# A two-layer graph attention block: the short last node tile spreads its two output halves over all four column groups of the array

## The chip, the cores and the metric

The kernel runs on one core of one Trainium2 chip. The metric is the device time of one execution in microseconds (us). Three runs of the kernel before gave 1805.76, 1805.07 and 1804.87 us: median 1805.07 us.

Short names used below: PE is TensorE (PEld its weight loads), DVE is VectorE, ACT is ScalarE, POOL is GpSimd, SP is SyncE, which only issues transfers here. A "row" of the profile is one line of it. A column group is a strip of 32 of the array's 128 columns; a matmul with up to 32 output rows occupies one strip, and its result lands in the 32 PSUM partitions of that strip.

## The reference

3125 nodes with 768 features, 53125 edges sorted by destination (25000 drawn ones in both directions and one self loop per node; the convolution adds a second self loop). All is fp32.

```python
h = relu(layernorm(x))
# layer 1: 4 heads of 256;  layer 2: 1 head of 768
def gat_conv(x, src, dst, W, a_src, a_dst, bias):
    xl = x @ W
    e = leaky_relu((xl @ a_src)[src] + (xl @ a_dst)[dst], 0.2)
    e = exp(e - segment_max(e, dst)[dst])
    alpha = e / (segment_sum(e, dst)[dst] + 1e-16)
    return segment_sum(xl[src] * alpha, dst) + bias
h1 = relu(layer_norm(gat_conv(h, W1 ...))) + h @ Wr1 + br1
h2 = layer_norm(gat_conv(h1, W2 ...)) + h1 @ Wr2 + br2
out = x + h2
```

## The kernel before

The nodes are cut into 25 tiles: tiles 0 to 23 have 128 nodes, tile 24 has the remaining 53 (`rows_of`, L116). The edges of a node tile lie in 17 slot tiles of 128 edges, of which tile 24 uses 8 (`tiles_of`, L122). A slot tile j feeds one or two quarters of the node tile, that is 32 nodes each (`QUARTERS`, L33), and the slot tiles are taken in five rounds (`ROUNDS`, L34). For tile 24 these are the slot tiles (0, 5), (1, 6), (4), (2) and (3, 7); only slot tile 4 feeds two quarters, so 9 pairs of slot tile and quarter are left, against 20 in a full tile.

**Before layer 1's sums.** Products x W1 are stored to the table `table1` in DRAM, attention weights and slot lists are made, and a part of h Wr1 is computed ahead. The first row gather of layer 1 is issued at 496.77 us of the span.

**Layer 1** (`sums`, L633 to L745, with `end1`, L1123 to L1176). POOL gathers one row of 4 KB per edge from `table1` by an indirect DMA per slot tile (L692). For each round PE multiplies the 0/1 placement, scaled by the attention weight (`w`, made on DVE at L712 and L713), with the gathered tile `g` and accumulates in the PSUM tile `pa` (L732): four column ranges of 256 per pair, the first two in one PSUM bank (`pa[:, 0]`), the last two in the next. After each round `step` advances the node tiles that are already summed: `finish` (L655; normalisation on DVE, L663 to L670, after a lag of three rounds) and then `end1`: layer norm (L1134 to L1138), transposes on PE (L1145, in `flip`), ReLU on ACT (L1150), adding of the residual on DVE (L1152), store of h1 to DRAM (L1159), and the dense product with W2 (L1164 to L1170), 8 steps of 128 rows of W2 by two output halves of 384 and 386 columns, each half in a PSUM tile `p2` of its own. ACT copies the halves into a row (L1173), DVE a pair of attention values (L1175), and SP stores the rows to `table2` (L1176, `store_rows` at L194). Dense products go through `by_columns` (L178), which issues a matmul per 32 output rows: 4 for a full tile, 2 (32 and 21 rows) for tile 24. The order on PE, DVE and ACT is the order in which the code is written (`manual_schedule`): in the last part of layer 1 the rounds of tile 24 alternate on PE with transposes and product of tile 22; then come tiles 23 and 24 with nothing between.

**Layer 2** (L1181 to L1421). No row of `table2` can be gathered before tile 24's rows are stored. POOL then gathers 3 KB rows (L1280), up to 36 slot tiles ahead (`RING`). For tile b the softmax needs all its slot tiles (`values`, L1293; `softmax`, L1304, with transposes `mix` at L1311 and L1325), then come five rounds of sums (`summed`, L1332; matmuls at L1347, two halves of 384 columns in two PSUM banks), then `finish` (L1352): DVE L1360 to L1367, with a square root on ACT (L480) in between, and the store of the output. Between the rounds PE works on the dense residual product h1 Wr2 (`residuals`, L1244; again `by_columns`, two halves of 384 columns in PSUM tiles `pr0`, `pr1`), which runs three tiles ahead of the sums: that of tile 24 is computed during the rounds of tile 21. On DVE, all of `finish(23)` stands ahead of `finish(24)`: the loop empties `ending` at its third round (L1406), and L1360 of the new tile follows at the fifth (L1410).

In the trace each fp32 matmul of the program stands as two rows (two passes): 3136 rows for the products with W2 are 2 x (24 x 64 + 32).

Of the kernel before, what the change touches and what calls it, by code (L numbers as in the profile page):

```python
# [68 lines left out]
def in_order(  # L69
# [108 lines left out]
    def by_columns(out_, lhsT, rhs, m, start, stop):  # L178

        for o in range(0, m, 32):  # L180
            e = min(o + 32, m)
            nc.tensor.matmul(out_[o:e], lhsT[:, o:e], rhs, start=start, stop=stop, skip_group_check=True)  # L182
# [450 lines left out]
    def sums(heads, cols, table, al, alo_d, ahead, lag, gp, ap, pp, end, more, pace, first=None, delay=0.0):  # L633
# [21 lines left out]
        def finish(b, own, pa):  # L655
            for _ in range(lag):
                yield

            r = rows_of(b)
            v = gp.tile([P, 2, heads], F32, name="aw", bufs=3)[:r]  # L660
            aw, share = v[:, 0], v[:, 1]
            ao = asked.pop(b)[:r]
            nc.vector.tensor_scalar(aw, ao[:, :heads, b], has[:r, 1, b:b + 1], has[:r, 2, b:b + 1],  # L663
                                    op0=OP.mult, op1=OP.max)
            nc.vector.scalar_tensor_tensor(share, ao[:, heads:, b], has[:r, 0, b:b + 1], aw, op0=OP.mult, op1=OP.add)
            nc.vector.tensor_scalar(share, share, 1e-16, None, op0=OP.add)
            nc.vector.reciprocal(share, share)
            z = gp.tile([P, width], F32, name="z", bufs=2)[:r]
            for o in range(0, width, n):
                nc.vector.scalar_tensor_tensor(z[:, o:o + n], own[:r, o:o + n], aw[:r, o // cols:o // cols + 1],  # L670
                                               pa[:r, o // f, o % f:o % f + n], op0=OP.mult, op1=OP.add)
            yield from end(b, z, share)
# [44 lines left out]
        with tc.manual_schedule(engines={PE, ACT, DVE}):  # L717
            ready = fetch(0, 0)
            for b in range(NB):
# [3 lines left out]
                for k, js in enumerate(ROUNDS):  # L723
# [5 lines left out]
                    for o in range(0, width, n):  # L729
                        for q, w, g in made:  # L730
                            to = (o // f, q)
                            nc.tensor.matmul(pa[32 * q:32 * q + 32, o // f, o % f:o % f + n], w[:, o // cols, :],  # L732
                                             g[:, o:o + n], start=to not in opened, stop=False,
                                             skip_group_check=True)
                            opened.add(to)
# [12 lines left out]
    with tc.tile_pool(name="m1", bufs=1) as mp:  # L748
# [320 lines left out]
        with tc.tile_pool(name="w2", bufs=1, reuse_waits="tile") as wp, tc.tile_pool(name="e1", bufs=2, reuse_waits="tile") as ep, \  # L1069
# [53 lines left out]
            def end1(b, z, share):  # L1123
# [47 lines left out]
                for pm, (o, n) in zip(pms, halves):  # L1171
                    m = min(n, C2 + 1 - o)
                    nc.scalar.activation(row[:, o:o + m], pm[:, :m], AF.Copy)  # L1173
                    if n > m:
                        nc.vector.tensor_copy(asad2[:r, b, :], pm[:, 384:n])  # L1175
# [5 lines left out]
    with tc.tile_pool(name="m2", bufs=1, reuse_waits="tile") as mp, \  # L1181
# [62 lines left out]
        def residuals():  # L1244

            for b in range(NB):
# [4 lines left out]
                pms = [pp.tile([P, 512], F32, name=f"pr{i}", bufs=2)[:r] for i in range(2)]  # L1251
                for k in range(NK2):
                    for i, pm in enumerate(pms):
                        by_columns(pm[:, :f], h1[:, k, :], wr2[:, k, i * f:(i + 1) * f], r,
                                   start=(k == 0), stop=(k == NK2 - 1))
# [3 lines left out]
                for i, pm in enumerate(pms):  # L1259
                    cs = slice(i * f, (i + 1) * f)  # L1260
                    nc.vector.tensor_add(xr[:r, cs], pm[:, :f], xr[:r, cs])
# [70 lines left out]
        def summed(b, k, pa, opened):  # L1332
# [12 lines left out]
            for i in range(2):  # L1345
                for q, w_, g in made:
                    nc.tensor.matmul(pa[32 * q:32 * q + 32, i, :f], w_, g[:, i * f:(i + 1) * f],  # L1347
                                     start=(i, q) not in opened, stop=False, skip_group_check=True)
                    opened.add((i, q))
            fetch()  # L1350

        def finish(b, pa):  # L1352
# [5 lines left out]
            for i in range(2):  # L1358
                cs = slice(i * f, (i + 1) * f)
                nc.vector.scalar_tensor_tensor(z[:, cs], own[:r, cs], v[:, 2:3], pa[:r, i, :f], op0=OP.mult, op1=OP.add)  # L1360
# [533 lines left out]
```

## Time and profile before

| | |
|---|---|
| median of three runs | 1805.07 us (1804.87 to 1805.76) |
| the profiled execution, its own time | 1801.14 us |
| its span, first to last instruction | 1799.2 us |
| mean granted TensorE clock | 0.965 |
| PE busy, 0 to 490 us (before the sums) | 471.7 us; DMA share 0.49 |
| PE busy, 490 to 1211 us (layer 1's sums) | 680.7 of 721 us; DMA share 0.96 |
| PE busy, 1211 to 1799 us (layer 2) | 484.9 of 588 us; DMA share 0.96 |
| POOL busy in layer 2 | 421.5 us, with 416 gathers |
| last gather of layer 1 issued, first of layer 2 | 1153.60 us and 1211.09 us |

How to read it: a row of a timeline has the start, the length, the engine, the line of the code, the operation with out<-in and its shape, the count of instructions merged into it, and in brackets how long the engine had been idle before it and whose end released it. In the table of windows each engine has busy time and, in brackets, its number of instructions; PEclk is the granted clock as a share of full speed. The last layer-2 gather is issued at 1764.93 us; the span ends with tile 24's output.

### The profile page before, as it was taken

To read this page: it belongs to the slowest core of one execution; us is meant where nothing else is said; L and a number is where in the kernel's file an instruction comes from. 1 tells how busy PE (TensorE), PEld (TensorE's weight loads), DVE (VectorE), ACT (ScalarE), POOL (GpSimd) and SP (SyncE) were. 2 spreads that over 40 slices of the span, in tenths; PEclk is the share of its full clock that TensorE was granted. 3 is DMA by queue.
4 is the path that set the end of the run, shared out by engine and by line. 5 is a ranking of instruction groups with operands and counts; after the bars stand their busy time and mean duration, and the time that the engine had idled before them with its cause. 6 is when DMAs were issued, how large, how long until landed. Compare 5 with 4: busy or idle time off the path is not lost. (4 is left out here: it accounts for less than half of the span.)

```text
span 1799.2 us, 43360 instructions
## 1 busy us (share of the span) xinstructions
PE 1637.3 (91%) x17747; PEld 870.2 (48%) x17747; DVE 998.1 (55%) x2639; ACT 454.1 (25%) x1286; POOL 885.9 (49%) x922
## 2 busy tenths in 40 slices
PE   8999999899968999999999999996988888888885
PEld 5666665566534555556554555532333333333331
DVE  7683443788865466566566565632444444444445
ACT  2222332000121222122122112122333333333342
POOL 2000111100055566666566666506777777777772
PEclk9999999999988999999999999998999999999997
DMA  7834546633199999999999999939999999999994
GB/s 239 275 104 136 147 114 192 233 131 123 36 341 407 381 407 407 409 405 410 406 400 411 411 398 400 401 104 387 367 387 380 376 386 386 372 386 384 378 345 148
DMA packets 173719, 562.56 MB, mean 313 GB/s; under 512 B 28610, under 2 KB 53976, under 8 KB 173384
## 3 DMA queue, kind: packets, MB, share of 16 engines
q0 software_dynamic: 100912, 402.06, 58.1%
q1 hardware_dynamic: 68206, 147.26, 23.0%
q10 hardware_dynamic: 4394, 10.39, 1.5%
q8 instruction: 142, 2.33, 0.5%
q14 instruction: 65, 0.53, 0.1%
HBM read 498.62 MB, written 65.62 MB: 314 GB/s over the span
## 5 line engine op out<-in xcount | busy, mean ns | idle before, releaser
L692 POOL DMA_INDIRECT g<-table,idx_s x416 | 407.6, 980 | 404.1 <-DVE m L613 174.7
L1280 POOL DMA_INDIRECT g<-table,idx_s x416 | 421.5, 1013 | 179.2 <-issue 63.7
L732 PE MATMUL pa<-g,w 128*32 128x256 f32 x3912 | 276.5, 389 | 32.0 <-DMA g<-table,idx_s 21.1
L182 PE MATMUL pr<-wr,h 128*32 128x384 f32 (+1 forms) x3136 | 292.4, 504 | 0.0
L182 PE MATMUL p<-w,h1T 128*32 128x384 f32 (+1 forms) x3136 | 283.9, 489 | 2.6 <-DVE h1T L1152 2.6
L732 PEld LDWEIGHTS pa<-g,w 128*32 128x32 f32 x3912 | 144.6, 112 | 146.1 <-issue 28.7
L1347 PE MATMUL pa<-g,w 128*32 128x384 f32 x1956 | 196.3, 509 | 3.1 <-DVE v L1372 3.1
L182 PEld LDWEIGHTS p<-w,h1T 128*32 128x32 f32 x3136 | 123.1, 110 | 125.6 <-issue 85.8
L713 DVE TENSOR_TENSOR w<-oh,al 128x128 f32<-128x128 f32 (+1 forms) x416 | 132.0, 317 | 80.4 <-PE pa L732 45.5
L182 PEld LDWEIGHTS pr<-wr,h 128*32 128x32 f32 (+1 forms) x3136 | 100.6, 112 | 151.0 <-issue 150.1
L1314 DVE CUSTOM_DVE_ANT_0 e<-mix,pen 128x640 f32<-128x640 f32 x25 | 20.6, 824 | 245.5 <-PE mix L1311 245.5
L182 PE MATMUL pr<-h0k,wr 128*32 128x256 f32 (+1 forms) x2304 | 146.9, 391 | 0.9 <-DMA h0k<-h0T_d 0.9
L837 PE MATMUL pm<-w,h0l 128*128 128x344 f32 (+1 forms) x468 | 140.8, 455 | 0.0
L1293 ACT ACTIVATE slots<-g 128x32 f32<-128x32 f32 x416 | 75.1, 222 | 231.4 <-DMA g<-table,idx_s 229.5
L974 PE MATMUL pm<-h0g,wr 128*128 128x512 f32 x288 | 131.7, 604 | 0.0
L837 PE MATMUL pm<-w,h0g 128*128 128x344 f32 x432 | 130.8, 459 | 0.3 <-ACT h0g L816 0.3
L905 POOL DMA_DIRECT2D hot_d<-ohd x25 | 13.4, 537 | 220.1 <-DVE own L491 121.0
L1347 PEld LDWEIGHTS pa<-g,w 128*32 128x32 f32 x1956 | 67.9, 116 | 110.5 <-issue 97.7
L712 DVE TENSOR_SCALAR oh<-iota_f,rel_s 128x32 f32<-128x32 f32 (+1 forms) x416 | 110.9, 267 | 0.1
L182 PEld LDWEIGHTS pr<-h0k,wr 128*32 128x32 f32 x2304 | 80.5, 111 | 55.0 <-issue 9.2
L837 PEld LDWEIGHTS pm<-w,h0l 128*128 128x128 f32 (+1 forms) x468 | 84.8, 185 | 44.1 <-issue 5.7
L1311 PE MATMUL mix<-ident,slots 128*128 128x128 f32 x125 | 22.5, 319 | 88.1 <-ACT slots L1293 88.1
(282 smaller groups left out, 1704.5 us busy)
## 6 DMA issues: line engine op xcount, KB each, us to landing
s<-slo_d SPq DMA_DIRECT2D x25, 544.0 KB
g<-table,idx_s POOLq DMA_INDIRECT x832
table<-row SPq DMA_DIRECT2D x24, 512.0 KB
own<-table SPq DMA_DIRECT2D x24, 512.0 KB
h1T_d<-h1T SPq DMA_DIRECT2D x24, 512.0 KB
h<-h1T_d SPq DMA_DIRECT2D x22, 512.0 KB
table<-row SPq DMA_DIRECT2D x24, 392.0 KB
ring<-in_x_dram SPq DMA_DIRECT2D x24, 384.0 KB
```

What stands on the lines that cost most here:

```text
L182: nc.tensor.matmul(out_[o:e], lhsT[:, o:e], rhs, start=start, stop=stop, skip_group_check=True)
L692: nc.gpsimd.indirect_dma_start(out=g, out_offset=None, in_=table[:, :], in_offset=bass.IndirectOffsetOnAxis(ap=idx_s[:, b * J + j:b * J + ...
L712: nc.vector.tensor_scalar(oh, iota_f[:, lo:hi], rel_s[:, c:c + 1], None, op0=OP.is_equal)
L713: nc.vector.tensor_tensor(w, oh[:, None, :].to_broadcast([128, heads, hi - lo]), al[:, POS[j], :, b:b + 1].to_broadcast([128, heads, hi - ...
L732: nc.tensor.matmul(pa[32 * q:32 * q + 32, o // f, o % f:o % f + n], w[:, o // cols, :], g[:, o:o + n], start=to not in opened, stop=False, ...
L837: nc.tensor.matmul(pm[:r, :C], h0[b][:, k, :], w1[:, k, i * C:(i + 1) * C], start=(k == 0), stop=(k == NK1 - 1))
L974: nc.tensor.matmul(pm, wr1[:, k, m * 128:(m + 1) * 128], groups[gi][:, k, :], start=(k == 0), stop=(k == NK1 - 1))
L1280: nc.gpsimd.indirect_dma_start(out=g, out_offset=None, in_=table2[:, :], in_offset=bass.IndirectOffsetOnAxis(ap=idx_s[:, b * J + j:b * J + ...
L1293: nc.scalar.activation(slots[b % 2][:, POS[j], :], gs[b, j][:, C2:C2 + 1].to_broadcast([128, 32]), AF.Copy)
L1311: nc.tensor.transpose(mix[:, c * 128:(c + 1) * 128], at[:, o:o + 4].rearrange("p q n -> p (q n)"), ident)
L1314: nc.vector.tensor_tensor_reduce(out=e, in0=mix[:, :WIN], in1=pen, scale=1.0, scalar=-BIG, op0=OP.add, op1=OP.max, accum_out=top)
L1347: nc.tensor.matmul(pa[32 * q:32 * q + 32, i, :f], w_, g[:, i * f:(i + 1) * f], start=(i, q) not in opened, stop=False, skip_group_check=True)
```

## The change

Tile 24 has 53 rows, so its matmuls use only the column groups 0 and 1. Its output halves are now told apart by place: half 0 stays at PSUM partitions 0 to 52, half 1 goes to 64 to 116, that is to the column groups 2 and 3. A helper gives the place, and `by_columns` takes an offset:

```diff
-    def by_columns(out_, lhsT, rhs, m, start, stop):
+    def by_columns(out_, lhsT, rhs, m, start, stop, at=0):
         for o in range(0, m, 32):
             e = min(o + 32, m)
-            nc.tensor.matmul(out_[o:e], lhsT[:, o:e], rhs, ...
+            nc.tensor.matmul(out_[at + o:at + e], lhsT[:, o:e], rhs, ...
+    def half_at(b, i):
+        o = 64 * i if rows_of(b) <= 64 else 0
+        return slice(o, o + rows_of(b))
```

It is used in four places: the sums of layer 1, the product with W2, the residual product with Wr2 and the sums of layer 2. The readers (DVE L670, L1175, L1261, L1360 and ACT L1173) take half 1 from partitions 64 to 116 of the same PSUM banks and write to partitions 0 to 52 as before.

```diff
# layer 1 sums (L729)
-                    for o in range(0, width, n):
+                    order = list(range(0, width, n))
+                    if rows_of(b) <= 64:
+                        order = [o + i * f for o in range(0, f, n) for i in range(2)]
+                    for o in order:
                         for q, w, g in made:
                             to = (o // f, q)
-                            nc.tensor.matmul(pa[32 * q:32 * q + 32, o // f, o % f:o % f + n], w[:, o // cols, :],
+                            p0 = 32 * q + half_at(b, o // f).start
+                            nc.tensor.matmul(pa[p0:p0 + 32, o // f, o % f:o % f + n], w[:, o // cols, :],
...
# product with W2 (L1164); the residual product (L1251) alike
-                pms = [pp.tile([128, 512], F32, name="p2", bufs=2)[:r] for _ in range(2)]
+                pms = [pp.tile([128, 512], F32, name="p2", bufs=2) for _ in range(2)]
                 for k in range(NK2):
-                    for pm, (o, n) in zip(pms, halves):
+                    for i, (pm, (o, n)) in enumerate(zip(pms, halves)):
                         by_columns(pm[:, :n], hT[:, k, :], w2[:, k, o:o + n], r,
-                                   start=(k == 0), stop=(k == NK2 - 1))
+                                   start=(k == 0), stop=(k == NK2 - 1), at=half_at(b, i).start)
...
# layer 2 sums (L1345)
-            for i in range(2):
-                for q, w_, g in made:
-                    nc.tensor.matmul(pa[32 * q:32 * q + 32, i, :f], w_, g[:, i * f:(i + 1) * f],
...
+            order = [(i, m) for i in range(2) for m in made]
+            if rows_of(b) <= 64:
+                order = [(i, m) for m in made for i in range(2)]
+            for i, (q, w_, g) in order:
+                p0 = 32 * q + half_at(b, i).start
+                nc.tensor.matmul(pa[p0:p0 + 32, i, :f], w_, g[:, i * f:(i + 1) * f],
```

The number and the shapes of all instructions stay the same. In both dense products the sequence on PE stays too (for each step half 0, then half 1), only the output partitions differ. In layer 1's sums the column ranges 0, 256, 512, 768 are taken as 0, 512, 256, 768; the sequence of slot tiles stays. Only layer 2's sums of tile 24 move visibly. On PE, at the end of the kernel, these rows stood before (g12 to g19 are the gathered slot tiles in the order of the rounds, w the weights, pa the sums; one row is one matmul or a run of like ones):

```order
L1347 MATMUL pa_18584<-g12_18334,w_18578 32x384
L1347 MATMUL pa_18584<-g13_18336,w_18578 32x384
L1347 MATMUL pa_18584<-g12_18334,w_18578 32x384
L1347 MATMUL pa_18584<-g13_18336,w_18578 32x384
L1347 MATMUL pa_18584<-g14_18388,w_18578 32x384
L1347 MATMUL pa_18584<-g15_18390,w_18578 32x384
L1347 MATMUL pa_18584<-g14_18388,w_18578 32x384
L1347 MATMUL pa_18584<-g15_18390,w_18578 32x384
L1347 MATMUL pa_18584<-g16_18392,w_18578 32x384 x4
L1347 MATMUL pa_18584<-g17_18394,w_18578 32x384 x2
```

And on PE in the same place after the change (L1360 is the new number of the line):

```order
L1360 MATMUL pa_18584<-g12_18334,w_18578 32x384 x2
L1360 MATMUL pa_18584<-g13_18336,w_18578 32x384 x2
L1360 MATMUL pa_18584<-g14_18388,w_18578 32x384 x2
L1360 MATMUL pa_18584<-g15_18390,w_18578 32x384 x2
L1360 MATMUL pa_18584<-g16_18392,w_18578 32x384 x4
L1360 MATMUL pa_18584<-g17_18394,w_18578 32x384 x2
```

The two halves of a pair now follow each other, where before both pairs of a round came for half 0 and then for half 1. DVE, ACT, POOL and SP keep their sequence everywhere.

More of the change, by code (lines that the diff above doesn't have):

```diff
@@ L1250, in residuals @@
                 r = rows_of(b)
-                pms = [pp.tile([P, 512], F32, name=f"pr{i}", bufs=2)[:r] for i in range(2)]
+                pms = [pp.tile([P, 512], F32, name=f"pr{i}", bufs=2) for i in range(2)]
                 for k in range(NK2):
@@ L1260, in residuals @@
                     cs = slice(i * f, (i + 1) * f)
[L1261 removed]
+                    nc.vector.tensor_add(xr[:r, cs], pm[half_at(b, i), :f], xr[:r, cs])
         fill = residuals()
```

20 lines of the change are left out of this document (11 added, 9 removed).

## The prediction

> **What bounds the kernel now.** I read the slices of the page first, to find where the transfers stop.
>
> ```profile
> PE   8999999899968999999999999996988888888885
> DMA  7834546633199999999999999939999999999994
> ```
>
> Through both layers' sums the DMA engines are at 9; between the layers there is one slice of 45 us at 3, and the last slice is at 4. Only there can less PE work shorten the span. The chain of waits that ended last crosses the gap as follows.
>
> ```profile
> 1196.34 0.39 DVE h1T L1152
> 1207.47 0.50 ACT row L1173
> 1207.98 0.32 SPq L196
> 1208.78 2.15 DMA hot<-hot_d
> 1211.09 7.56 DMA g<-table,idx_s
> ```
>
> Tile 24's h1T, its product with W2 (10.32 us of PE, quoted next), the eviction, the store, and then the first gather of layer 2, for which POOL has waited 45 us:
>
> ```profile
> 1211.09 1.00 POOL L1280 DMA_INDIRECT g<-table,idx_s  x1 [45.13 <-DMA hot<-hot_d]
> ```
>
> The timeline of PE over the end of layer 1 shows an engine that is nearly never idle:
>
> ```profile
> 1154.77 1.85 PE L732 MATMUL pa<-g,w 128*32 128x256 f32 x28
> ...
> 1159.09 1.68 PE L732 MATMUL pa<-g,w 128*32 128x256 f32 x14
> 1160.70 1.09 PE L1145 MATMUL p<-ident,z 128*128 128x128 f32 x8
> 1161.73 3.43 PE L732 MATMUL pa<-g,w 128*32 128x256 f32 x30
> ...
> 1165.13 4.13 PE L182 MATMUL p<-w,h1T 128*32 128x384 f32 x46
> 1169.09 1.67 PE L732 MATMUL pa<-g,w 128*32 128x256 f32 x7
> ...
> 1174.52 1.86 PE L732 MATMUL pa<-g,w 128*32 128x256 f32 x14
> ...
> 1182.24 12.26 PE L182 MATMUL p<-w,h1T 128*32 128x384 f32 x128 [1.57 <-DVE h1T L1152]
> ...
> 1196.78 10.32 PE L182 MATMUL p<-w,h1T 128*32 128x384 f32 x62 [1.01 <-DVE h1T L1152]
> ```
>
> The first row is the last round of tile 23. The rows at 1159.09, 1161.73, 1169.09 and 1174.52 are tile 24's rounds (the second holds two), with tile 22's transposes and product between them; then follow the products of tiles 23 and 24. So PE's own order sets the time from 1159 to 1207, and what comes off it there brings the first gather forward. From there the kernel is held by POOL and the transfers, which start earlier by the same amount.
>
> At the end of the span I read PE and DVE together:
>
> ```profile
> 1760.32 1.33 PE L1311 MATMUL mix<-ident,slots 128*128 128x128 f32 x5 [7.25 <-ACT slots L1293]
> ...
> 1768.62 4.08 PE L1347 MATMUL pa<-g,w 128*32 128x384 f32 x48 [1.18 <-DVE v L1372]
> ...
> 1779.29 8.33 PE L1347 MATMUL pa<-g,w 128*32 128x384 f32 x36 [1.97 <-DVE v L1372]
> ```
>
> ```profile
> 1784.74 1.02 DVE L1367 SCALAR_TENSOR_TENSOR z<-z,bn_rs,xr 128x768 f32<-128x768 f32 x1
> 1787.67 1.13 DVE L1360 SCALAR_TENSOR_TENSOR z<-own,v,pa 53x384 f32<-53x384 f32 x2 [1.91 <-PE pa L1347]
> ```
>
> The last sums of tile 24 take 8.33 us, and DVE waits for them, but for only 1.91 us: just before, it finished tile 23.
>
> **The change part by part.** First the rate of two and of four column groups. Tile 24's product is 64 instructions in 10.32 us: 161 ns each. Four groups, on the same count and shape:
>
> ```profile
> 1432.38 5.30 PE pr L182 x64
> ```
>
> 83 ns each, half. In the sums of 256 columns two groups need (3.43 - 0.38) / 29 = 105 ns from start to start (the last one's own 0.38 us taken off), four need (1.85 - 0.38) / 27 = 54 ns. In these full rounds each group already streams a gathered tile of its own, and in a full product half 0 of one bank and half 1 of the other follow without a gap; what no row shows is both banks written by different groups throughout. So I take the four-group rate for tile 24; the bounds are that rate and no gain at all.
>
> *Product of tile 24 (L1164):* 10.32 us becomes 64 x 83 ns = 5.30 us, **5.0 us less**. Nothing hides it: PE waited for the h1T just ahead of it and ACT waits for its end. The second half of h1T, made right behind the first, is needed only after four of the eight steps. The product of tile 24 starts at full clock (last row), that of tile 23 did not (first rows):
>
> ```profile
> 1183.00:1183.50 0.50, 0.50 (x8) 0.28 (x8) 0.50 (x1) 0.00 (x0) 0.00 (x0) 0.50 0.00 0
> 1186.00:1186.50 0.50, 0.50 (x8) 0.13 (x4) 0.50 (x2) 0.00 (x0) 0.00 (x0) 0.84 0.00 0
> 1197.00:1202.00 5.00, 5.00 (x32) 1.57 (x30) 0.40 (x2) 0.46 (x2) 0.00 (x0) 1.00 0.21 43
> ```
>
> The column before the last two is the granted clock. About 3.5 us at 0.50 fell into tile 23's product after PE had idled 1.57 us, which cost about 1.75 us. [...]
>
> *Layer 1's sums of tile 24 (L732):* 72 instructions. 64 go from 105 to 54 ns, 8 (the round of slot tile 2, one quarter) from 210 to 105: 4.1 us of PE. Not all is on the path. The first round ends 0.8 us earlier, and so tile 22's transposes; its ReLU and add take their time behind them:
>
> ```profile
> 1162.99 0.69 DVE L1152 TENSOR_TENSOR h1T<-h1T,r1t 128x512 f32<-128x512 f32 x1 [2.21 <-ACT h1T L1150]
> ```
>
> This ends at 1163.68, 2.98 us after the transposes began; with these at 1159.9 it ends at 1162.9, and PE is through the next two rounds at 1160.9 + 1.7 = 1162.6. The product of tile 22 starts at 1162.9 instead of 1164.8: 1.9 us. The other two rounds stand between parts of that product with nothing to wait for: 0.85 us each. Sum **3.6 us**; bounds 1.7 (the last two rounds alone) and 4.1.
>
> *Layer 2's sums of tile 24 (L1347):* three full rounds take 4.08 us for 48 rows, 85 ns each. With four groups 32 rows need 2.7 us, the 4 of slot tile 2 need 0.7: 3.4 us at full clock. Now the clock:
>
> ```profile
> 1780.00:1781.00 1.00, 1.00 (x6) 0.26 (x4) 0.97 (x2) 0.00 (x0) 0.00 (x0) 0.54 0.35 128
> 1783.00:1784.00 1.00, 1.00 (x8) 0.40 (x6) 0.37 (x2) 0.58 (x2) 0.00 (x0) 0.75 0.00 0
> ```
>
> Half speed from about 1780.1 to 1783.5: 1.7 us more, so 5.1 us and an end at 1784.4; all of it at half speed, 6.8 us and 1786.1. But L1360 can't start before DVE has ended L1367 of tile 23, at 1784.74 + 1.02 = 1785.76, and nothing in that chain waits for tile 24's sums. So DVE is late next: from 1787.67 to 1785.76, **1.9 us less** of PE's 3.2; bounds 1.6 and 1.9. [...]
>
> *Residual product of tile 24 (L1251):* the same 32 matmuls, 5 us less of PE, during tile 21's rounds at 1738 to 1749. Cover: PE idles 7.25 us ahead of 1760.32 for gathered rows, and POOL issues them without a break, 17 rows with 0.30 us between, of which these are the first and the last:
>
> ```profile
> 1743.46 0.95 POOL L1280 DMA_INDIRECT g<-table,idx_s  x1 [0.30 <-PE pa L1347]
> 1764.93 1.73 POOL L1280 DMA_INDIRECT g<-table,idx_s  x1 [0.30 <-ACT e L1320]
> ```
>
> Taken as **0**; if the 0.30 us ahead of a gather was a wait for a freed buffer after all, two steps of 0.65 us between tile 21's rounds give up to 1.3 us.
>
> *Readers from partitions 64 to 116:* no row shows such a read. Five rows of about 0.5 us; two lie on the path between the layers and one at the end. I take the time unchanged, by the same operation at equal size; were they twice as long, 1.5 us.
>
> Sum: 5.0 + 3.6 + 1.9 = **10.5 us**. The profiled execution took 1801.14 us, 1.94 over its span and 3.93 below the median; the span's parts are the same in either, so I take the sum off both: 1790.6 there, **1794.6 us** for the median. A measurement can tell about 0.2% of this kernel, 3.6 us, from no change.
>
> **Rivals.**
> 1. *The half-clock stretch moves:* it covers tile 24's product as well (a burst of 5.3 us after 2.3 us with hardly more than transposes), 1.75 us more: 1796.3. Or tile 23's goes: 1792.9. The rows above show both behaviours after like pauses. 15% and 8%.
> 2. *The last rounds of layer 1 become bound by gathered rows:* then only product and end gain, 6.9 us: 1798.2. Against it: the last gather is issued 20 us before the last round,
>
> ```profile
> 1153.60 1.01 POOL L692 DMA_INDIRECT g<-table,idx_s  x1 [0.30 <-issue]
> ```
>
>    and one took 7.56 us from issue to landing at 1211.09, so the rows lie there by about 1162, also for a round that comes at 1171. 6%.
> 3. *Four groups overlap less here than in full tiles.* If a half of the gain were lost in product and sums of layer 1, 4.3 us: 1798.9. Against it: 161 to 83 ns. [...] The trace's ratio of 1.94 decides. 7%.
> 4. *The halves don't overlap at all* (two banks at once): 1805.1. 3%.
> 5. *Layer 2 gives the earlier start back,* since it is held elsewhere: only the end gains, 1803.2. Against it: the chain runs from the first gather on through gathers. 4%.
> 6. *Slower: a drain at each switch between the group pairs.* An instruction lasts 489 ns while its group is free again after 4 x 83 = 332: if a pair had to run empty before the other begins, some 0.16 us per switch, and nothing overlapped, 16 switches in the product, 20 in layer 1's sums and 18 in layer 2's would add 54 x 0.16 = 8.6 us: 1813.7. It shows as slower from 0.07 us per switch. Against it: full tiles change group with every instruction at 83 ns. 2%.
>
> ```profile
> L182 PE MATMUL p<-w,h1T 128*32 128x384 f32 (+1 forms) x3136 | 283.9, 489 | 2.6 <-DVE h1T L1152 2.6
> ```
>
> **How the numbers follow.** The forecast as summed has 55%. The range goes down to 1791.0 (tile 23's half-clock stretch gone and the residual's 1.3 us) and up to 1798.5 (rivals 1 and 2, or the sums' lower bound with a stretch more); outside are rivals 3 to 6, 16%. Faster by over 0.2%: forecast and rivals 1 to 3, 91%; within 0.2%: 4 and 5, 7%; slower: 2%.
>
> **What would show it.** In the new profile: tile 24's product 5.3 us at full clock (not 10.3); its four groups of layer-1 rows at about 0.9, 1.7, 0.9 and 0.9 us; the first layer-2 gather 8.6 us earlier, at about 1202.5, and the last one as much earlier; tile 24's last sums 3.4 to 6.8 us, and L1360 of 53 rows right behind L1367 with no idle before it. Wrong it would be if the product stayed above 8 us, if the first gather moved by less than 5 us, or if the stretch from first to last gather grew by what was won.

## The result and the profile after

The changed kernel took 1795.59 us (median of 20 runs) against 1804.27 us (20 runs) for the kernel before on the same chip: ratio 0.9952, 95% interval 0.9936 to 0.9968, so 5.8 to 11.5 us less, in the middle 8.7. Forecast were 1794.6 us and 10.5 us less. One of the 20 runs of the changed kernel took 2390.15 us at a granted clock of 0.653 (the others 1788.34 to 1804.30 us); the ratio and its interval leave it out. The profiled execution of the changed kernel took 1797.35 us, with a span of 1795.4 us and a mean granted clock of 0.961.

First PE over the end of layer 1, in the timeline after the change (start, length, line, operation, count, idle time before it). L742 are layer 1's sums, L1155 the transposes, L182 the dense products.

```profile
1164.94 1.21 PE L742 MATMUL pa<-g,w 128*32 128x256 f32 x13
1166.08 1.09 PE L1155 MATMUL p<-ident,z 128*128 128x128 f32 x8
1167.10 1.93 PE L742 MATMUL pa<-g,w 128*32 128x256 f32 x32
1169.11 4.12 PE L182 MATMUL p<-w,h1T 128*32 128x384 f32 x48
...
1181.45 1.45 PE L1155 MATMUL p<-ident,z 128*128 128x128 f32 x8
1184.47 12.29 PE L182 MATMUL p<-w,h1T 128*32 128x384 f32 x128 [1.57 <-DVE h1T L1162]
...
1199.03 7.05 PE L182 MATMUL p<-w,h1T 128*32 128x384 f32 x62 [1.02 <-DVE h1T L1162]
```

From tile 24's first round (first row) to the transposes of tile 23 (1181.45) it is now 16.51 us. In the trace of before the same stretch ran from 1159.09 to 1179.21, 20.12 us: 3.61 less. In before, the first rows of tile 22's product and the transposes of tile 23 stand here:

```profile
1164.79 0.52 PE L182 MATMUL p<-w,h1T 128*32 128x384 f32 x2
1179.21 1.45 PE L1145 MATMUL p<-ident,z 128*128 128x128 f32 x8
```

Tile 22's product now begins 4.17 us after the first round. Before, its first two rows began 5.70 us after it. So this inner step is 1.5 of the 3.61 us, counted from the first rows as in the forecast, which had 1.9. The product of tile 24 is at 7.05 us, not at 5.3. The table of windows says why; the column behind the bracket is the granted clock:

```profile
1197.00:1198.00 1.00, 0.65 (x8) 1.00 0.00 0
1199.00:1202.00 3.00, 2.97 (x18) 0.50 0.30 73
1202.50:1206.00 3.50, 3.50 (x50) 1.00 0.00 0
```

18 rows in 3 us at half clock, 50 in 3.5 us at full clock (a few of them belong to the product that follows). This was the first rival: the stretch of half clock fell into tile 24's product, and another had already fallen into tile 23's (a granted clock of 0.54 from 1185.0 to 1188.4; 12.29 us, for 12.26 before).

The first gather of layer 2, on POOL:

```profile
1210.22 1.00 POOL L1290 DMA_INDIRECT g<-table,idx_s  x1 [40.43 <-DMA hot<-hot_d]
```

From the start of tile 24's product to this gather it is 11.19 us, before 14.31. The gather itself comes only 0.87 us earlier in its span, because in this execution tile 24's first round began 5.85 us later (1164.94 for 1159.09). Up to there the two programs are the same instructions, and over all profiled executions of this study on normal chips that round began between 1158.86 and 1166.78 us. So I compare stretches, not times in the span. Counted from tile 24's first round, the gather comes after 45.28 us instead of 52.00.

The end, first PE, then DVE:

```profile
1758.13 1.33 PE L1321 MATMUL mix<-ident,slots 128*128 128x128 f32 x5 [9.46 <-ACT slots L1303]
...
1777.37 3.42 PE L1360 MATMUL pa<-g,w 128*32 128x384 f32 x36 [1.97 <-DVE v L1386]
```

```profile
1782.82 1.02 DVE L1381 SCALAR_TENSOR_TENSOR z<-z,bn_rs,xr 128x768 f32<-128x768 f32 x1
1783.76 1.23 DVE L1373 SCALAR_TENSOR_TENSOR z<-own,v,pa 53x384 f32<-53x384 f32 x2
```

Tile 24's last sums take 3.42 us for 8.33, this time at a granted clock of 1.00 (before 0.79). DVE's first step of the 53-row tile (L1373) follows tile 23's last (L1381) with no idle time; before it had waited 1.91 us. From the start of these sums to that step it is 6.39 us, before 8.38. The first row shows 9.46 us idle ahead of tile 23's softmax, for 7.25 before.

The readers of partitions 64 to 116 take hardly longer each. Groups by line and form, after (mean ns is the second number behind the bar):

```profile
L675 DVE SCALAR_TENSOR_TENSOR z<-own,aw,pa 53x256 f32<-53x256 f32 x4 | 1.7, 472 | 0.0
L1183 ACT ACTIVATE row<-p 53x385 f32<-53x385 f32 x1 | 0.5, 490 | 0.0
```

and before:

```profile
L670 DVE SCALAR_TENSOR_TENSOR z<-own,aw,pa 53x256 f32<-53x256 f32 x4 | 1.6, 466 | 0.0
L1173 ACT ACTIVATE row<-p 53x385 f32<-53x385 f32 x1 | 0.5, 488 | 0.1
```

But where two DVE readers follow each other, the pair takes 0.1 us longer: the 53-row step above lasts 1.23 us, as in every trace with this place changed, and 1.13 us in before, as in every trace without. The second instruction starts 0.61 us after the first, behind its end, where it started 0.53 us after it before. That is 0.1 us on the path at the end of the kernel. In layer 1 the four readers together take 1.77 us for 1.63, under tile 23's product, where PE doesn't wait for them.

The whole span adds up: 5.85 later at the first round, 3.61 less in the rounds, 3.12 less from product to gather (14.31 to 11.19), and 2.93 less from the first gather to the end (588.11 to 585.18) make 3.81 less; 1799.2 to 1795.4 us are 3.8.

### The profile page after: what moved, and what is told of

Read it like the earlier page. It is cut to its first block, busy times and chain, and to the rows that moved or that the text cites. A ratio compares the mean times of both kernels' runs of the same rounds, so it can differ in the third digit from the quotient of the medians.

```text
span 1795.4 us, 43359 instructions
## 1 busy us (share of the span) xinstructions
PE 1626.8 (91%) x17747; PEld 877.3 (49%) x17747; DVE 996.7 (56%) x2639; ACT 453.4 (25%) x1286; POOL 883.6 (49%) x922
## 5 line engine op out<-in xcount | busy, mean ns | idle before, releaser
L742 PE MATMUL pa<-g,w 128*32 128x256 f32 x3912 | 278.0, 393 | 32.2 <-DMA g<-table,idx_s 20.2
L182 PE MATMUL pr<-wr,h 128*32 128x384 f32 (+1 forms) x3136 | 290.3, 509 | 0.0
L182 PE MATMUL p<-w,h1T 128*32 128x384 f32 (+2 forms) x3136 | 283.5, 492 | 2.7 <-DVE h1T L1162 2.6
L742 PEld LDWEIGHTS pa<-g,w 128*32 128x32 f32 x3912 | 148.3, 113 | 142.5 <-issue 29.1
L1360 PE MATMUL pa<-g,w 128*32 128x384 f32 x1956 | 186.6, 503 | 3.1 <-DVE v L1386 3.1
L182 PEld LDWEIGHTS p<-w,h1T 128*32 128x32 f32 (+1 forms) x3136 | 125.5, 111 | 120.9 <-issue 79.8
L182 PEld LDWEIGHTS pr<-wr,h 128*32 128x32 f32 (+1 forms) x3136 | 103.0, 113 | 145.7 <-issue 136.6
L182 PE MATMUL pr<-h0k,wr 128*32 128x256 f32 (+1 forms) x2304 | 147.2, 391 | 0.7 <-DMA h0k<-h0T_d 0.7
L1360 PEld LDWEIGHTS pa<-g,w 128*32 128x32 f32 x1956 | 65.8, 115 | 107.4 <-issue 93.9
L182 PEld LDWEIGHTS pr<-h0k,wr 128*32 128x32 f32 x2304 | 81.1, 111 | 54.0 <-issue 9.0
```

Source lines behind the costliest of these rows:

```text
L182: nc.tensor.matmul(out_[at + o:at + e], lhsT[:, o:e], rhs, start=start, stop=stop, skip_group_check=True)
L742: nc.tensor.matmul(pa[p0:p0 + 32, o // f, o % f:o % f + n], w[:, o // cols, :], g[:, o:o + n], start=to not in opened, stop=False, skip_gr ...
L1360: nc.tensor.matmul(pa[p0:p0 + 32, i, :f], w_, g[:, i * f:(i + 1) * f], start=(i, q) not in opened, stop=False, skip_group_check=True)
```

## The experiments

Theory: layer 1's end and tile 24's product are PE time on the path, layer 2 starts earlier by what they give, the residual product is covered by idle time, and DVE caps the gain at the end. The rivals: a part doesn't pay, or another part pays in its place. Runs of one group share the runs of the kernel before. The four kernels with one place each ran on a chip where the kernel before took about 2099 us instead of 1805, and so did, on another such chip, three of the later ones: half 0 whole before half 1, the product twice and the residual product twice. The traces taken there have lower transfer rates (268 to 270 GB/s for 314 over the span) and PE often idle between single matmuls (up to 1.98 us at a time early in layer 2 of the kernel with the product alone); so from those runs I take ratios and the stretches between the layers and at the end, never times.

### One place at a time

Each of these four kernels keeps the new placement in one of its four places. Undone in the others (here the residual product and layer 2's sums):

```diff
-                                   start=(k == 0), stop=(k == NK2 - 1), at=half_at(b, i).start)
+                                   start=(k == 0), stop=(k == NK2 - 1))
...
-                    nc.vector.tensor_add(xr[:r, cs], pm[half_at(b, i), :f], xr[:r, cs])
+                    nc.vector.tensor_add(xr[:r, cs], pm[:r, :f], xr[:r, cs])
...
-            if rows_of(b) <= 64:
-                order = [(i, m) for m in made for i in range(2)]
...
-                p0 = 32 * q + half_at(b, i).start
+                p0 = 32 * q
```

Only layer 1's sums:

> Only the sums of layer 1 have tile 24's second half on the idle column groups; both dense products and layer 2's sums are as before. Theory (PE's own order sets the time there): from tile 24's first sums to tile 23's transposes 16.5 us instead of 20.1, as in the changed kernel; tile 24's product about 10.3 us (up to 12.0 if a half-clock stretch falls into it); last sums about 8 us. Time: 3.6 us less, ratio 0.998. Rival (these sums were covered by gathered rows, and the 3.6 us of the two traces came from chance): 19 to 20 us for that stretch, time unchanged.

Ratio 0.9969 (0.995 to 0.9988). PE's timeline:

```profile
1315.99 1.13 PE L742 MATMUL pa<-g,w 128*32 128x256 f32 x16
...
1332.41 1.45 PE L1155 MATMUL p<-ident,z 128*128 128x128 f32 x8
...
1348.31 11.92 PE L182 MATMUL p<-w,h1T 128*32 128x384 f32 x62 [1.01 <-DVE h1T L1162]
```

16.42 us from the first round to the transposes (the first row here holds all 16 rows of that round), against 20.34 to 20.58 in the three kernels that keep the old sums, counted alike from the first of the 16. From tile 22's transposes to those of tile 23, where the traces agree to 0.02 us, it is 15.35 against 18.51; in the change and in before it was 15.37 and 18.51. So the whole 3.6 us belongs to this place. The product, here in the old placement, took 11.92 us, since half clock fell into it (0.57 on average from 1348 to 1352).

Only the product with W2:

> Only the product of tile 24 with W2 has its second half on the idle groups. Theory: product 5.3 us at full clock, 7.05 us if a half-clock stretch of 3.4 us begins with it, as in the changed kernel's trace; the first gather of layer 2 comes 5.0 or 3.3 us earlier after the product's start (9.3 or 11.2 us instead of 14.3); time 5.0 or 3.3 us less, ratio 0.997 to 0.998. Rival (four groups on two banks don't overlap fully): 7 us at a granted clock of 1.00 throughout.

Ratio 0.9984 (0.9963 to 1.0004): by time alone no more than a hint. The rows decide, first PE's timeline, then the first gather:

```profile
1354.79 5.47 PE L182 MATMUL p<-w,h1T 128*32 128x384 f32 x60 [1.01 <-DVE h1T L1160]
...
2078.95 6.64 PE L1356 MATMUL pa<-g,w 128*32 128x384 f32 x36 [1.97 <-DVE v L1382]
```

```profile
1364.56 1.00 POOL L1288 DMA_INDIRECT g<-table,idx_s  x1 [44.95 <-DMA hot<-hot_d]
```

9.77 us from the product's start to the gather; with the old product it was 14.31 in before, 14.29 and 14.56 in the two next kernels. So this place gives 4.5 to 4.8 us on the path, not 5.0. The second row is news: the last sums, unchanged here, took 6.64 us and not 8.33, and DVE then had almost nothing to wait for. In before 3.4 us at 0.50 stand in the 8.33 us and cost 1.7 of them; so 6.64 us is full clock, an estimate by length, as for the last sums of all runs from here on. DVE's row:

```profile
2085.64 1.13 DVE L1369 SCALAR_TENSOR_TENSOR z<-own,v,pa 53x384 f32<-53x384 f32 x2 [0.22 <-PE pa L1356]
```

Only the residual product:

> Only the residual product of tile 24 with Wr2 has its second half on the idle groups. Theory (gathers are issued without a break there, and PE then idles for gathered rows): PE idles about 9.5 instead of 7.3 us before the transposes of tile 23's softmax, from the first gather to the end 588 us as before, time unchanged, ratio 1.000. Rival (PE's release of buffers sets the pace of the gathers): 1.3 us less from the first gather to the end, ratio 0.999.

Ratio 0.9987 (0.9966 to 1.0009), which holds 0 and 1.3 us alike: not decided by this run. The idle time ahead of tile 23's softmax, which was to tell, can't be read on this chip: it is 0.79 us there, in which nothing that the profile shows was waited for. Its last sums show the other case again, the 8.33 us of half clock and the long wait of DVE, 1.91 us:

```profile
2083.61 8.33 PE L1356 MATMUL pa<-g,w 128*32 128x384 f32 x36 [1.98 <-DVE v L1382]
```

```profile
2092.00 1.13 DVE L1369 SCALAR_TENSOR_TENSOR z<-own,v,pa 53x384 f32<-53x384 f32 x2 [1.91 <-PE pa L1356]
```

Only layer 2's sums:

> Only the sums of layer 2 have tile 24's second half on the idle groups. Theory (DVE's work on tile 23 caps the gain): last sums 3.4 us at full clock (5.1 with a half-clock stretch) instead of 8.3, and the first DVE instruction of tile 24's ending right behind tile 23's last, no idle; time 1.9 us less, ratio 0.999, whatever the clock. Rival (PE alone sets the end): the end moves by all that the sums lose, 3.2 to 4.9 us, ratio 0.997 to 0.998.

Ratio 0.9993 (0.9973 to 1.0013). PE, then DVE:

```profile
2078.88 3.42 PE L1358 MATMUL pa<-g,w 128*32 128x384 f32 x36 [1.98 <-DVE v L1384]
```

```profile
2084.34 1.02 DVE L1379 SCALAR_TENSOR_TENSOR z<-z,bn_rs,xr 128x768 f32<-128x768 f32 x1
2085.27 1.23 DVE L1371 SCALAR_TENSOR_TENSOR z<-own,v,pa 53x384 f32<-53x384 f32 x2
```

From the start of the last sums to the 53-row step: 6.39 us here, 6.69 with the old sums at full clock, 8.39 with the old sums at half clock. The longer reader pair takes 0.1 us of that back: the last DVE step ends 12.49 us after the sums' start here, 12.69 us with the old sums at full clock, 14.38 at half clock. The cap is as forecast, but the gain is 0.2 us or 1.9 us, and which of them a run gets depends on where a stretch of half clock falls.

### The change again, and two ways to go on from it

> The changed kernel once more, for a second trace and as a base for the two kernels beside it. Theory (a half-clock stretch of about 3.4 us falls where it happens to fall): from tile 24's first sums to tile 23's transposes 16.5 us as in the first trace, but tile 24's product either 5.5 us at full clock or 7.0 us, and tile 23's either 10.6 or 12.3; ratio 0.994 to 0.998. Rival (the shorter burst itself brings the clock down): the product 7.0 us again.

1793.62 us (6 runs), ratio 0.993 (0.9903 to 0.9958). PE, with no half clock between the layers this time (a granted clock of 1.00 from 1176.4 to 1204.4), and the first gather:

```profile
1194.67 5.46 PE L182 MATMUL p<-w,h1T 128*32 128x384 f32 x60 [1.01 <-DVE h1T L1162]
...
1771.56 4.98 PE L1360 MATMUL pa<-g,w 128*32 128x384 f32 x36 [1.98 <-DVE v L1386]
```

```profile
1204.45 1.00 POOL L1290 DMA_INDIRECT g<-table,idx_s  x1 [34.51 <-DMA hot<-hot_d]
```

9.78 us from product to gather, as with the product alone. By their length, 4.98 us for 3.42, the stretch of half clock came into the last sums, and the 53-row step still stood 6.40 us behind their start: the cap covers it. First gather to end: 585.15 us, as in the first trace (585.18).

Next, tile 24's normalised sums of layer 1 are turned (transposed) two steps earlier, so that its transposes and ReLU lie inside tile 23's product; they get PSUM of their own:

```diff
-            for _ in range(lag):
+            for _ in range(lag if b < NB - 1 else lag - 2):
...
+                spare = pp.tile([P, 2, 512], F32, name="pa", bufs=2) if b == NB - 1 else None
...
+                        pt = spare[:, k0 // 4].rearrange("p (k n) -> p k n", n=128)
...
-                pms = [pp.tile([128, 512], F32, name="p2", bufs=2) for _ in range(2)]
+                pms = [pp.tile([128, 512], F32, name="p2" if b < NB - 1 else "pr", bufs=2) for _ in range(2)]
```

> As the changed kernel, but tile 24 runs two steps less behind tile 23, so that its transposes stand on PE ahead of the last two of eight steps of tile 23's product; transposes and product take other PSUM buffers (pa, pr), so that they need no eviction of tile 23. Theory (the pause for transposes, ReLU and add of tile 24 is on the path): tile 24's product follows tile 23's without a pause and at full clock, 5.5 us; from the start of tile 23's product to the first gather of layer 2 20.6 us (22.6 with the changed kernel at full clock), 2.0 us less than the changed kernel, 3.7 less where a half-clock stretch fell into its product. Rival (eviction or DVE sets the path): no change against the changed kernel.

1791.42 us (6 runs), ratio 0.9922 (0.9894 to 0.9949). PE:

```profile
1179.20 8.01 PE L182 MATMUL p<-w,h1T 128*32 128x384 f32 x96 [1.57 <-DVE h1T L1167]
1187.57 0.70 PE L1160 MATMUL pa<-ident,z 53*128 53x53 f32 x8 [0.36 <-DVE z L1148]
1188.20 2.80 PE L182 MATMUL p<-w,h1T 128*32 128x384 f32 x32
1190.81 5.37 PE L182 MATMUL pr<-w,h1T 128*32 128x384 f32 x64
```

The first gather came at 1200.34 us: 21.14 us from the start of tile 23's product, against 22.64 in the change repeated. 1.5 us less, forecast were 2.0: 1.25 us of it because the product of tile 24 now starts with no idle time (11.61 us after tile 23's instead of 12.86), 0.25 behind that; 0.36 us of waiting for DVE is new. The times of the two kernels can't be told apart, their intervals overlap.

Third, on top of it, DVE's work on tile 24's end up to the statistics is put ahead of the last three instructions of tile 23 (statistics of tile 24 in tiles of their own):

```diff
-                    if k == 2:
+                    if k == 2 and b < NB - 1:
...
-                        ending = finish(b, pa)
+                        before, ending = ending, finish(b, pa)
                         next(ending)
+                        if b == NB - 1:
+                            next(ending)
+                            next(ending)
+                            for _ in before:
+                                pass
```

> As the kernel with the early transposes, and at the end DVE does the first half of tile 24's ending (sums out of PSUM, statistics) ahead of tile 23's last three instructions. Theory (DVE caps the end): with the last sums at full clock, 3.4 us, tile 24's first DVE instruction starts when PE ends, about 3 us earlier than in the changed kernel, and the last DVE instruction ends 1.3 us earlier; with a half-clock stretch in the last sums nothing is won (0.2 us lost). Rival (the store of tile 23, now later, or the ACT in between sets the end): the span ends no earlier.

1792.21 us (6 runs), ratio 0.9923 (0.9895 to 0.9952). PE and DVE at the end:

```profile
1770.81 5.11 PE L1365 MATMUL pa<-g,w 128*32 128x384 f32 x36 [1.97 <-DVE v L1391]
```

```profile
1776.00 1.23 DVE L1378 SCALAR_TENSOR_TENSOR z<-own,v,pa 53x384 f32<-53x384 f32 x2 [2.55 <-PE pa L1365]
...
1782.58 1.01 DVE L1386 SCALAR_TENSOR_TENSOR z<-z,bn_rs_l,xr 53x768 f32<-53x768 f32 x1
```

By their 5.11 us, half clock fell into the sums; DVE waited 2.55 us for them with tile 23's steps now behind, and its last step ended 12.78 us after the sums' start; in the change repeated, also at half clock, 12.49. So the other order loses 0.3 us in this case; the case at full clock, where it could gain, didn't come up.

### Is it the order or the place?

In layer 1's sums the change alters the placement and the order of the column ranges. I believed that a matmul that waits for a busy column group holds up those behind it, so that the order was needed too. The two reorderings are taken out, the placement stays:

```diff
-                    if rows_of(b) <= 64:
-                        order = [o + i * f for o in range(0, f, n) for i in range(2)]
...
-            if rows_of(b) <= 64:
-                order = [(i, m) for m in made for i in range(2)]
```

> As the changed kernel in where the halves go, but both sums in the order of before: in layer 1 column ranges 0, 256, 512, 768 instead of 0, 512, 256, 768; in layer 2 all pairs of a round for half 0, then for half 1. Theory (matmuls start in program order, so one that waits for its group holds up the next): in layer 1 three instead of two turns per round, 18.3 us from tile 24's first sums to tile 23's transposes (16.5 changed, 20.1 before); in layer 2 no difference, since two pairs already name four groups, 3.4 us at full clock. Rival (a matmul for an idle group passes one that waits): 16.5 us.

One run, 1788.07 us. The stretch from the first round (1158.86) to the transposes of tile 23 (1175.36) was 16.50 us, the same as with the new order (16.51), and the last sums took 3.43 us. My theory of this run fell: the placement does it alone. How far can a matmul for an idle group get past waiting ones? In the next kernel tile 24's product takes all eight steps of half 0 first, then all of half 1:

```diff
-                for k in range(NK2):
-                    for i, (pm, (o, n)) in enumerate(zip(pms, halves)):
+                steps = [(k, i) for k in range(NK2) for i in range(2)]
+                if rows_of(b) <= 64:
+                    steps = [(k, i) for i in range(2) for k in range(NK2)]
+                for k, i in steps:
...
```

> The changed kernel, but tile 24's product with W2 takes all eight steps of half 0 (column groups 0 and 1) first and then all eight of half 1 (groups 2 and 3). Asked: how far a matmul for an idle column group gets past earlier ones that wait for a busy group. Theory A, none passes: two groups at a time, 64 x 161 ns = 10.3 us for the product, as in the kernel before. Theory B, each group takes its own next matmul from anywhere behind: 5.3 to 5.5 us, as in the changed kernel. Theory C, a short look-ahead of a few matmuls: only the seam in the middle overlaps, 9 to 10.2 us. Half clock in the stretch would add up to 1.75 us to any of them.

On the second of the slower chips the product ran from 1352.42 to 1363.40, 10.98 us, with half clock for its first 3.2 us (0.52), which costs 1.5 us: some 9.4 us at full clock, theory C. The groups by form in the window 1358.0 to 1359.4, at the seam (384 columns are half 0, 386 are half 1):

```profile
L182 PE MATMUL p<-w,h1T 128*32 128x386 f32 x5 | 1.8, 491 | 0.0
L182 PE MATMUL p<-w,h1T 128*21 128x386 f32 x5 | 1.8, 490 | 0.0
L182 PE MATMUL p<-w,h1T 128*21 128x384 f32 x5 | 1.8, 485 | 0.0
L182 PE MATMUL p<-w,h1T 128*32 128x384 f32 x5 | 1.8, 485 | 0.0
```

Between 1357.0 and 1357.9 there were only rows of 384 columns, from 1359.8 on only of 386. So half 1 began about 1.3 us before half 0 was through, and no earlier: its first two rows start at 1358.02, while six rows of half 0 start only between 1358.33 and 1358.98. A matmul got past a few waiting ones (six rows), not past a whole half (32 rows). So the matmuls did not all start in program order: 386-column ones started at 1358.02, while 384-column ones ahead of them started up to 0.96 us later. In a round of layer 1's sums the old order has at most four matmuls (eight rows, of which two start at once) ahead of the second half, which is within that reach.

### Doses: the product twice, the residual product two and three times

```diff
-                    for i, (pm, (o, n)) in enumerate(zip(pms, halves)):
+                    for again in range(2 if b == NB - 1 else 1):
+                        for i, (pm, (o, n)) in enumerate(zip(pms, halves)):
...
-                                   start=(k == 0), stop=(k == NK2 - 1), at=half_at(b, i).start)
+                                       start=(k == 0 and again == 0), stop=(k == NK2 - 1), at=half_at(b, i).start)
```

> The changed kernel, but each step of tile 24's product with W2 is issued twice (its sums count twice, so the later values differ). Theory (all of this product lies on the path that opens layer 2, and layer 2 gives nothing back): the product takes 10.7 to 11 us in place of 5.4 (1.7 more where half clock falls in), tile 23's product to the first layer-2 gather 28 us in place of 22.6, from there to the end 585 to 586 us as before, so 5.3 us longer in all. Rival (layer 2 is held by something that doesn't start with that gather): from the first gather to the end 580 to 583 us.

```profile
1350.13 10.65 PE L182 MATMUL p<-w,h1T 128*32 128x384 f32 x124 [1.01 <-DVE h1T L1162]
```

The first gather came at 1365.09: 14.96 us from the product's start, 5.18 more than 9.78. Twice the product costs its full length up to the gather. What follows the gather can't be read on this chip: 740.81 us here, 722.44 in the kernel that takes half 0 whole, 728.37 in the next one.

The residual product is doubled by the same edit (`for again in range(2 if b == NB - 1 else 1)` around its `by_columns`):

> The changed kernel, but each step of tile 24's residual product with Wr2 is issued twice (the product of that tile counts twice in the output). Theory (PE's idle time before tile 23's softmax, 8 to 9.5 us, covers it): PE works 2.8 to 3 us longer during tile 21's rounds, the idle time before the transposes of tile 23's softmax becomes 5 to 6.5 us, and the time from the first layer-2 gather to the end stays 585 to 586 us. Rival (those rounds are on the path, through the buffers that their gathered rows free): that time becomes 588 us, and the idle time stays.

On that chip PE waited between single matmuls there (0.59 and 0.23 us, for nothing that the profile shows) and had no idle time left ahead of tile 23's softmax, so this says nothing. On a normal chip, three times (`range(3 ...)`):

> The changed kernel, but each step of tile 24's residual product with Wr2 is issued three times (the product of that tile counts three times in the output). [...] Theory (PE's idle time before tile 23's softmax covers this product): PE works 5.5 us longer during tile 21's rounds, the idle time of 8 to 9.5 us becomes 2.5 to 4, and the time from the first layer-2 gather to the end stays 585 to 586 us. Rival (those rounds are on the path, since they free the buffers of the gathered rows): that time becomes 590 to 592 us and the idle time stays.

I sized the dose wrongly in both: one residual product of tile 24 is 64 rows of 83 ns, 5.3 us, so two more add 10.6 us, not 5.5. PE, and the first gather:

```profile
1747.54 7.96 PE L182 MATMUL pr<-wr,h 128*32 128x384 f32 x92
...
1760.42 0.77 PE L1322 MATMUL mix<-ident,slots 128*128 128x128 f32 x5 [0.40 <-ACT slots L1304]
```

```profile
1209.03 1.01 POOL L1291 DMA_INDIRECT g<-table,idx_s  x1 [37.60 <-DMA hot<-hot_d]
```

The idle time fell from 8.25 us (the change repeated) to 0.40, and the time from the first gather to the end (1797.5 us) rose to 588.47, by 3.3 us. So idle time took up some 7 us of the 10.6, and 3.3 came through. The cover is real, but its edge is near.

## Why the prediction was right, and where it was off

**The bound.** That less PE work between the layers and in the last 20 us shortens the span was right: tile 24's rounds, its product and the first gather moved as whole stretches, and doubling the product moved the gather by its full length. Taken by place in the span, the first gather moved by only 0.87 us, less than the 5 us under which the prediction called itself wrong. Counted from tile 24's first round, it comes 6.72 us earlier, and 9.82 us in the repeat (after 42.18 us), where no half clock fell between the layers; forecast were 8.6. Rival 5 (layer 2 gives it back) fell: first gather to end took 588.11 us before, and 585.18, 585.15 and 585.08 in the change, its repeat and the kernel with the old order.

**Layer 1's sums, 3.6 us:** 3.61 in the first trace and 3.61 in the repeat (16.51 us from 1162.27 to 1178.78). The part alone shows that nothing else causes it. Its inner steps fit less well than the sum: the first round ends 0.46 us earlier, not 0.8 (1.36 us from its first row to tile 22's transposes, before 1.82), and what comes behind the start of tile 22's product gives 2.1 us, not 1.7, when counted from that product's first row. That these two miss in opposite ways is luck.

**The product, 5.0 us:** 4.5 on the path (14.31 to 9.78 from its start to the first gather). The rate is right, 5.46 us for 60 rows; but its last four rows stand among those of the next product, and the last starts 5.63 us in:

```profile
1200.28 0.49 PE L182 MATMUL pr<-wr,h 128*32 128x384 f32 x2
1200.30 0.49 PE L182 MATMUL p<-w,h1T 128*32 128x386 f32 x2
```

At 0.33 us from start to start, the last of 16 rows of a group should start 4.9 us in. Groups 2 and 3 run 0.73 us behind from their first row on: half 0 starts at 1194.67, half 1 at 1195.40. PE's weight loads in the repeat show what for, and so do ACT's ReLUs of tile 24:

```profile
1195.40 0.15 PEld L182 LDWEIGHTS p<-w,h1T 128*32 128x32 f32 x8 [0.59 <-ACT h1T L1160]
1192.95 2.40 ACT L1160 ACTIVATE h1T<-p,be_c,g_c 128x53 f32<-128x53 f32 x8
```

Half 1 sums in one of the two `p2` buffers, the one that held the second four transposes, and that isn't free until ACT has read the last of them, at 1195.35. In each of the seven traces with the changed product in this order half 1's first row starts 0.05 us behind the end of that ReLU. Before, it cost some 0.1 us, an estimate: half 1's first weights were loaded at 1197.51, 0.74 us behind half 0's (1196.77) and behind the same ReLU, but half 0's two rows per group, at 0.33 us each, took 0.66 us of that. The prediction looked at the second half of h1T, but not at this buffer. In the kernel that turns tile 24 early, transposes and product have other PSUM tiles; there the halves start 0.01 us apart and the product takes 5.37 us. From its start to the first gather it is 9.53 us, only 0.25 less than 9.78: both halves now end together, and ACT copies them one behind the other (1196.24 to 1197.24), where half 0's copy had run under half 1's last rows. In the first trace of the change the half clock took another 1.4 us of this term: rival 1, which was given 15%.

**The end, 1.9 us: the mis-sized term.** The step "half speed from about 1780.1 to 1783.5" was read from one trace and taken as belonging to the kernel. It doesn't: the old last sums took 8.33 us in before and in one part kernel, 6.64 in the others, and then DVE waits only 0.22 us. From the start of the sums to the last DVE step the change takes 12.49 us, at full and at half clock, before 14.38 or 12.69: the term is 1.9 us when before hits the half clock and 0.2 when it doesn't, which is far below the lower bound of 1.6. That the first pair of traces gives the 1.9 of the forecast is luck of the clock. The cap by DVE was right and holds in every trace of the changed end that keeps DVE's order; none of them has the new sums at half clock throughout, as the bound of 1.6 took them (3.42 to 5.11 us instead of 6.8).

**The residual product, 0 (up to 1.3):** not settled. The idle time behind it grew from 7.25 to 9.46 us, so most of what it saved went there, as argued. But from the first gather to tile 23's softmax it was 549.23 us before and is 547.91 in the first trace (1210.22 to 1758.13), 1.3 less, and behind that 38.88 against 37.27, 1.6 less. The dose run shows that the first of these stretches answers to that product once the idle time is used up, so the 1.3 us may be its share; one trace of before on a normal chip can't tell them from scatter: in the repeat, the old order and the two kernels that go on from it, this stretch is 546.86 to 548.45 us.

**The readers, 0:** 472 against 466 ns and 490 against 488 ns for one, but 0.1 us for the pair of the 53-row step at the end; it is in the 12.49 us above.

Sum as measured: 3.6 + 4.5 + 0.2 to 1.9 are 8.3 to 10.0 us at full clock in tile 24's product, with up to 1.3 more from the residual product. The runs say 8.7 (5.8 to 11.5), the repeat 0.993 of 1807.1 us, 12.6 (7.6 to 17.5). That 1795.59 us lies within 1 us of the 1794.6 forecast is partly chance: the gain was 1.8 us smaller, and the kernel before was 0.8 us faster here than in its first three runs. The drain at each switch (rival 6) isn't there: the product of four groups would not reach 5.4 us with it.

The lowest ratio with an interval is that of the kernel that also turns tile 24 early: 0.9922 (0.9894 to 0.9949) against 0.993 for the change, which the times can't tell apart. Its 1.5 us stand in the trace, not yet in the times.

## What to carry to other kernels

When a short last tile leaves column groups idle, split what it computes over them by output partitions; it pays where PE's order alone sets the time, here between two layers (3.6 and 4.5 us), and hardly where another engine is late next (0.2 us at the end when before has full clock there). Give each operation its own stretch (from what starts it to who waits for it) and compare stretches, since the same program started the same round anywhere within 8 us. Work that starts earlier can meet a wait that was hidden before, as half 1 met the buffer that ACT still read (0.73 us): look up what each operand and each PSUM tile waits for at the new start. A stretch of half clock seen in one trace is not a property of the place (the old last sums took 8.33 us in two traces, 6.64 in two): cost a term with and without it, and name both.

## What was not expected of the hardware

- Matmuls for an idle column group passed a few waiting ones (six rows): the old order of layer 1's rounds cost nothing (16.50 against 16.51 us), while a whole half in front left only some 1.3 us of overlap.
- The stretches of half clock, some 3.4 us each where the granted clock was read (1780.1 to 1783.5 us in before, 1198.9 to 1202.4 in the first trace after), fell into tile 23's product (12.26 us for 10.60), tile 24's product (7.05 for 5.46, 11.92 for 10.32), the last sums (8.33 for 6.64, 4.98 for 3.42), or none of these, in kernels with the same PE program there.
- On two chips the kernel before took 2099 us. PE's timeline in layer 2, of the kernel that takes half 0 whole before half 1, reads there like this, "issue" being time in which nothing that the profile shows was waited for:

```profile
1384.21 1.44 PE L182 MATMUL pr<-wr,h 128*32 128x384 f32 x2 [1.30 <-issue]
1387.03 1.53 PE L182 MATMUL pr<-wr,h 128*32 128x384 f32 x3 [1.38 <-issue]
```

What holds PE up there isn't shown by any run here.
